# A two-layer graph transformer on one core: chain tiles, one standing PSUM tile, and sums by identity products

## The chip, the cores and the metric

The kernel runs on one core of a Trainium2 chip. The metric is the device time of one execution in microseconds, with all operands and the result in device memory. A matrix engine (TensorE, PE in the profile), a vector engine (VectorE, DVE), an activation engine (ScalarE, ACT), GpSimd (POOL) and the queues of SyncE (SP) work side by side, each in its own order, and wait for one another by semaphores. Tiles lie in SBUF or in PSUM; PSUM has eight banks of 512 floats per partition, and matrix products land there.

## The reference

2500 nodes with 128 features and one of 16 types, 40,000 edges with one of 32 types. Two layers of typed attention, a linear output with bias, the old features added, and a last normalisation:

```python
k, q, v = typed_linear(x, ntype, Wk | Wq | Wv).reshape(n, H=8, HS=16)
kT = einsum('nhd,htdo->nhto', k, Watt)      # every node, every edge type
vT = einsum('nhd,htdo->nhto', v, Wmsg)
a  = einsum('ehd,ehd->eh', kT[src, :, etype], q[dst]) * pri[:, etype].T / 4
att = edge_softmax(a, dst, n)               # over the edges of one target node
hag = segment_sum(vT[src, :, etype] * att[:, :, None], dst)
h = silu(typed_linear(hag, ntype, Wa)) * alpha + x * (1 - alpha)
x = (h - mean) / sqrt(var + 1e-5) * g + b   # end of a layer
out = layernorm(x0 + x @ ff_w + ff_b)       # after both layers
```

A typed linear takes for each node the matrix of the node's type.

## The kernel before

**Preparation.** The edges are ranked by target and type on the chip, and the nodes are sorted by in-degree into 49 blocks of 128. In a block every node has as many slots as the largest in-degree there (25, 21, 19, ... 11 in four classes of four node types, and 42 (written TOP; 26 own slots and a remainder that several rows share), 20, 16, 14, 9 for a mixed rest of all types). A table in DRAM, `tab`, holds one row of k and v (256 floats) per node and edge type.

**A layer** is `edges(l)`. For every slot of a block POOL issues one indirect DMA (L1528) that gathers 128 rows of the table, one for each node of the block. Four slots fill one chunk, a `kv` tile of [128, 4, 256]; there are twelve such tiles, and a gather waits until the chunk that used its tile twelve chunks ago has been read for the last time. When a chunk has landed, DVE multiplies its k half by the block's query (L1544, "kk") and sums over each head (L1550), which gives the scores `a`. When all chunks of a block have their scores, the generator `finished` does the rest in steps, mixed into the chunks of the next block (three steps to a chunk): mask, maximum and subtraction on DVE, exp on ACT, the sum of the weights (`den`), then for every chunk v times weight and the addition to `acc`, and last a reduction of `acc` over its four slots to `sums`.

In layer 0 query and `acc` lie in SBUF and the weights in one PSUM bank (`hold`). In layer 1 the query is copied by ACT (L1353) into a double bank of the pool `tps`, where the weights and `acc` lie as well; the profile calls that tile `tb`.

**Superblocks.** Up to four blocks form a superblock. After its last block `nodes` follows: normalise the sums, typed linear, tanh, skip and layer norm. A typed linear takes DVE masks (`masked`: xm = (type == t) x h^T) and a PE product for each type, into a PSUM bank of the pool `nps` (tiles `nb`). In layer 0 `nodes` also makes k, v and q of the next layer and then `table_block`, which makes the second layer's table rows: PE products (L354) into double banks of `tps`, copies to `st` tiles by ACT and DVE (L362, L360), and a scatter by POOL (L1761). In layer 1 it makes the output rows, which POOL scatters (L1793). `queries0` makes the queries of the next superblock in layer 0; `queries1` loads them in layer 1.

**Order.** POOL's order is that of the program: gathers and scatters as written. For DVE, ACT and PE a scheduler keeps the program's order nearly, with hints by which nothing is pulled ahead of the chunk at hand (`Held`; instructions issued through it all have line 267 in the profile). `spread` and `tick` hand out the steps of `nodes`, of the queries and of the tables to the slots: so many steps for so many slots, where the number of steps is written in the program. A scatter is put behind by eight steps (`late`).

PSUM before: one bank for `nps`, one for `hold`, three double banks for `tps`, eight banks in all.

## Time and profile before

| | |
|---|---|
| median of 3 runs | 3025.17 us (3024.95 to 3028.88) |
| the profiled execution's own time | 3024.62 us |
| its span, first to last instruction | 3022.8 us |
| preparation | 0 to 590 us |
| layer 0, first to last gather | 590 to 1803 us |
| passage: last rows of the second table | 1803 to 1874.6 us |
| layer 1 | 1874.6 to 2976.5 us |
| tail after the last gather | 2976.5 to 3022.8 us |
| busy over the span | PE 52%, DVE 63%, ACT 32%, POOL 67% |

Times are read against the execution's own 3024.62 us; the 1.8 us beside the span lie before the first and after the last instruction. A row of the groups gives line, engine, operation, tile written <- tiles read, shapes, count, then busy us, mean ns, and the idle time just ahead of these instructions with what ended it. In a row of the timeline the bracket at the end is the idle time ahead. "issue" means that nothing the profile shows was waited for. A PE product in float32 has two records.

### The profile page before, as it was taken

The numbers are of one execution on the slowest core, as the hardware profiler recorded it, in microseconds if no ns is written. First come the engines' busy times: TensorE is split into PE (matmuls) and PEld (weight loads), VectorE is DVE, ScalarE is ACT, GpSimd is POOL, SyncE is SP. The second block draws the span as 40 slices with busy tenths as digits, with TensorE's granted clock in tenths as the row PEclk, the third lists the DMA queues.
The fourth block names the chain that finished last, engine by engine and source line by source line (L and its number), as shares of the span: only waits on it lengthen the run. The fifth ranks groups of instructions, "written<-read, shape, count | busy, mean of one in ns | idle before, by whom it ended". The sixth has DMA issues, their size and how long they took to land.

```text
span 3022.8 us, 21562 instructions
## 1 busy us (share of the span) xinstructions
PE 1580.5 (52%) x5325; PEld 703.1 (23%) x5325; DVE 1891.1 (63%) x4383; ACT 978.7 (32%) x1635; POOL 2032.2 (67%) x2116
## 2 busy tenths in 40 slices
PE   5999978413667667777777884021122213221212
PEld 2445434201223322332223332010111001000001
DVE  7467655257657766777666653476576667666665
ACT  3887533200434234434444553011111111111111
POOL 3333665477777777777777762777677777777773
PEclk9999777556777777787777786555555556555555
DMA  7999999943677577867788897333334333333331
GB/s 217 416 418 418 394 392 397 371 107 100 234 275 260 197 248 282 297 225 254 271 303 296 330 354 278 105 110 111 92 103 118 111 111 109 112 109 106 106 100 45
DMA packets 163485, 671.37 MB, mean 222 GB/s; under 512 B 52012, under 2 KB 78926, under 8 KB 138302
## 3 DMA queue, kind: packets, MB, share of 16 engines
q0 software_dynamic: 113152, 635.19, 58.6%
q1 hardware_dynamic: 34218, 27.57, 3.3%
q10 hardware_dynamic: 15976, 7.10, 1.0%
q8 instruction: 46, 0.75, 0.1%
q14 instruction: 93, 0.76, 0.1%
HBM read 245.42 MB, written 425.02 MB: 222 GB/s over the span
## 4 chain that ended last, share of the span: by engine, by line
POOL 24%; issue 17%; DMA 16%; DVE 13%; PE 7%; ACT 3%; ACTq 0%; DVEq 0%; POOLq 0%
POOL kv L1528 21%; DMA kv<-tab,ell 14%; PE nb L267 6%; DVE kv L1544 2%; DVE xm L267 2%; PE tb L354 2%; DVE kv L267 2%; DMA tab<-st,row 2%; DVE a L1550 1%; DVE acc L267 1%; ACT L267 1%; POOL tab L1761 1%; DVE tb L267 1%; DVE hs L267 1%; POOL out_dram L1793 1%
## 5 line engine op out<-in xcount | busy, mean ns | idle before, releaser
L1528 POOL DMA_INDIRECT kv<-tab,ell x1638 | 1615.6, 986 | 542.6 <-issue 437.4
L362 ACT COPY st<-tb 128x512 f32<-128x512 f32 (+1 forms) x984 | 681.6, 777 | 535.4 <-PE tb L354 349.8
L1544 DVE TENSOR_TENSOR kv<-kv,tb 128x512 f32<-128x512 f32 (+3 forms) x223 | 142.7, 640 | 381.1 <-DMA kv<-tab,ell 367.4
L1544 DVE TENSOR_TENSOR kv<-kv,q 128x512 f32<-128x512 f32 (+3 forms) x223 | 142.9, 643 | 324.6 <-DMA kv<-tab,ell 316.1
L354 PE MATMUL tb<-bdv,vT 32*128 32x512 f32 x784 | 266.0, 781 | 45.0 <-ACT st L362 41.5
L1550 DVE TENSOR_REDUCE a<-kv 128x32 f32<-128x512 f32 (+3 forms) x446 | 280.8, 632 | 1.3
L354 PE MATMUL tb<-bdv,kvT 32*128 32x512 f32 x784 | 253.7, 790 | 22.9 <-ACT st L362 22.5
L354 PE MATMUL tb<-bdk,kvT 32*128 32x512 f32 x784 | 257.3, 776 | 7.9 <-ACT st L362 7.3
L267 PE MATMUL nb<-xm,wa 128*128 128x384 f32 (+2 forms) x336 | 178.0, 690 | 148.8 <-DVE xm L267 144.2
L267 PE MATMUL nb<-xm,wkqv 128*128 128x384 f32 (+2 forms) x504 | 218.6, 583 | 48.0 <-DVE xm L267 37.0
L1168 POOL DMA_INDIRECT tab<-st,rows x98 | 101.8, 1039 | 197.7 <-ACT st L362 169.4
L360 DVE COPY st<-tb 128x512 f32<-128x512 f32 (+1 forms) x192 | 128.7, 707 | 145.3 <-PE tb L354 74.7
L267 PE MATMUL nb<-by,all_rows 49*128 49x512 bf16 (+2 forms) x30 | 13.3, 442 | 381.6 <-DVE by L267 353.5
L354 PE MATMUL tb<-bdk,kT 32*128 32x512 f32 x784 | 210.6, 785 | 1.7 <-issue 1.6
L267 PE MATMUL nb<-ident,hag 128*128 128x128 f32 x98 | 24.6, 385 | 284.1 <-DVE hag L267 276.4
L1761 POOL DMA_INDIRECT tab<-st,row x98 | 106.1, 1083 | 80.4 <-DVE st L360 28.0
L267 PEld LDWEIGHTS nb<-xm,wkqv 128*128 128x128 f32 x504 | 106.4, 223 | 174.8 <-issue 88.6
L267 PEld LDWEIGHTS nb<-xm,wa 128*128 128x128 f32 x336 | 85.9, 272 | 240.6 <-issue 184.3
L267 DVE TENSOR_TENSOR tb<-kv,tb 128x512 f32<-128x512 f32 (+3 forms) x216 | 138.2, 640 | 0.2
L267 PE MATMUL nb<-xm,wq 128*128 128x384 f32 (+2 forms) x168 | 92.0, 708 | 87.2 <-DVE xm L267 87.1
L354 PEld LDWEIGHTS tb<-bdv,vT 32*128 32x128 f32 x784 | 98.8, 226 | 147.7 <-ACT st L362 118.9
L1353 ACT COPY tb<-hq 128x128 f32<-128x128 f32 x49 | 13.0, 267 | 369.4 <-DVE sums L267 268.8
(348 smaller groups left out, 2519.9 us busy)
## 6 DMA issues: line engine op xcount, KB each, us to landing
kv<-tab,ell POOLq DMA_INDIRECT x1638
hq<-hqx SPq DMA_DIRECT2D x7, 768.0 KB, 4.8
hqx<-hs SPq DMA_DIRECT2D x7, 512.0 KB, 3.5
hq<-hqx SPq DMA_DIRECT2D x5, 576.0 KB, 4.9
hqx<-xr SPq DMA_DIRECT2D x10, 256.0 KB, 19.2
hqx<-hs SPq DMA_DIRECT2D x5, 384.0 KB, 3.2
hr<-hqx SPq DMA_DIRECT2D x7, 256.0 KB, 5.6
tab<-st,rows POOLq DMA_INDIRECT x98
```

The lines of the kernel that those rows point to most:

```text
L267: put = issue(*args, **kwargs)
L354: stream[nc.tensor] = nc.tensor.matmul(pt[:, b], yT[s, i * P:(i + 1) * P], bd[s, tt, :], start=True, stop=True)
L360: nc.vector.tensor_copy(to, pt)
L362: stream[nc.scalar] = nc.scalar.copy(to, pt)
L1168: put = nc.gpsimd.indirect_dma_start(out=tabs[0].rearrange("(n t) c -> n (t c)", t=16), out_offset=bass.IndirectOffsetOnAxis(ap=rows1[:, t ...
L1353: nc.scalar.copy(pair[:, 1, :D], got[s][0][:, i, :])
L1528: get = nc.gpsimd.indirect_dma_start(out=kv[:, j - j0, :], out_offset=None, in_=tabs[l][:], in_offset=bass.IndirectOffsetOnAxis(ap=ell[:, ...
L1544: stream[nc.vector] = nc.vector.tensor_tensor(kk, kk, of.unsqueeze(1).to_broadcast([P, c, D]), op=ALU.mult)
L1550: nc.vector.tensor_reduce(to, kk.rearrange("p k (h d) -> p k h d", h=H), axis=AX.X, op=ALU.add)
L1761: put = nc.gpsimd.indirect_dma_start(out=tabs[1].rearrange("(n t) c -> n (t c)", t=16), out_offset=bass.IndirectOffsetOnAxis(ap=row2[:, tg ...
L1793: put = nc.gpsimd.indirect_dma_start(out=out, out_offset=bass.IndirectOffsetOnAxis(ap=node[:, b:b + 1], axis=0), in_=o[:, i, :], in_offset ...
```

## The change

PSUM is dealt out anew: two banks for `nps` (before, one), two double banks for `tps` (before, three), and one standing tile `held` of two banks for both layers. Its first bank is `acc`; its second holds the weights in front and two places for queries, used in turn, behind.

- Both layers: ACT copies the block's query into `held` (L1351; in layer 0 this is a new copy); exp writes the weights there. The widest block keeps its weights in SBUF, but its sums go to `held` too.
- Layer 0: `acc` moves from SBUF to `held`; DVE still multiplies and adds.
- Layer 1: DVE multiplies v by the weights in place, chunk by chunk, and PE adds up: a product of the chunk with the identity into `held`, with start at the block's first chunk and stop at its last. DVE's additions are gone.
- `linear_of` no longer copies h^T to SBUF for a mixed superblock: the masks read PSUM.
- In layer 0's mixed superblocks k, v and q are made in two passes over the masks, (k, v) and (q), where it was three.
- The steps handed to `spread` go from 58 extra to 41, from 14 to 13, and from 25 to 24.

```diff
--- before.py
+++ after.py
@@ -315,11 +315,6 @@
         types = list(types)
-        if len(types) > TC:
-            h2 = pool.tile([P, SB * P], F32, name="h2", tag="hb")
-            on.scalar.copy(h2[:, :n], hT[:, :n])
-            yield
-            hT = h2
         some, ps = 2 if len(types) > TC else TC, None
         for t0 in range(0, len(types), some):
             xms = list(masked(pool, types[t0:t0 + some], ntb, hT, n))
@@ -1214,10 +1209,14 @@
         eps = npl.tile([P, 1], F32, name="eps")
         nc.vector.memset(eps, LN_EPS)
-        nps = ctx2.enter_context(tc.tile_pool(name="nps", bufs=1 if fast else 5, space=PSUM))
-
-        hold_ps = ctx2.enter_context(tc.tile_pool(name="hold", bufs=1, space=PSUM)) if fast else None
-        tps = ctx2.enter_context(tc.tile_pool(name="tps", bufs=3, space=PSUM))
+        nps = ctx2.enter_context(tc.tile_pool(name="nps", bufs=2 if fast else 5, space=PSUM))
+
+        turn, held = [0], None
+        if fast:
+            hold_ps = ctx2.enter_context(tc.tile_pool(name="hold", bufs=1, space=PSUM))
+            held = hold_ps.tile([P, 2, SB * P], F32, name="held")
+            assert max(OWN, *KB[:TOP], *KB[TOP + 1:]) * H <= 2 * D
+        tps = ctx2.enter_context(tc.tile_pool(name="tps", bufs=2 if fast else 3, space=PSUM))
         sbs = []
@@ -1347,22 +1346,20 @@
             def query(s, i):
-                if l == 0:
-                    return got[s][0][:, i, :], None
-                pair = tps.tile([P, 2, SB * P], F32, name="tb")
-                nc.scalar.copy(pair[:, 1, :D], got[s][0][:, i, :])
-                return pair[:, 1, :D], pair
-
-            def moved(pair, by, what, to):
+                at = (2 + turn[0] % 2) * D
+                turn[0] += 1
+                nc.scalar.copy(held[:, 1, at:at + D], got[s][0][:, i, :])
+                return held[:, 1, at:at + D]
+
+            def moved(by, what, to):
                 n = what.shape[1]
-                ps = pair[:, 1, D:D + n] if pair is not None else tps.tile(
-                    [P, 2, SB * P], F32, name="tb")[:, 0, :n]
+                ps = tps.tile([P, 2, SB * P], F32, name="tb")[:, 0, :n]
                 nc.tensor.matmul(ps, by, what, start=True, stop=True)
                 nc.scalar.copy(to, ps)
-            def finished(s, i, chunks, kvt, a, pair, sums, den):
+            def finished(s, i, chunks, kvt, a, sums, den):
                 i0, k, _ = sbs[s]
@@ -1371,7 +1368,7 @@
                 rest = None
                 if i0 + i == TOP:
                     rest, chunks = kvt[-1], chunks[:-1]
-                    moved(pair, node_of, rest[:, 3, :RK * REST * H],
+                    moved(node_of, rest[:, 3, :RK * REST * H],
                           a[:, OWN:K, :].rearrange("p k h -> p (k h)"))
                     yield
                 on.vector.tensor_tensor(
@@ -1386,24 +1383,29 @@
                 yield
                 w = av
                 if rest is None:
-                    if l == 0:
-                        held = hold_ps.tile([P, SB * P], F32, name="hold")
-                    w = (pair[:, 1, D:D + K * H] if l else held[:, :K * H]).rearrange(
-                        "p (k h) -> p k h", h=H)
+                    w = held[:, 1, :K * H].rearrange("p (k h) -> p k h", h=H)
                 on.scalar.activation(w, av, AF.Exp)
                 if rest is not None:
-                    moved(pair, rows_of, a[:, OWN:K, :].rearrange("p k h -> p (k h)"),
+                    moved(rows_of, a[:, OWN:K, :].rearrange("p k h -> p (k h)"),
                           rest[:, 3, :RK * REST * H])
                 yield
                 yield
                 on.vector.tensor_reduce(den[:, i, :], w.rearrange("p k h -> p h k"),
                                         axis=AX.X, op=ALU.add)
-                if rest is None and l:
-                    acc = pair[:, 0].rearrange("p (k c) -> p k c", k=CH)
-                else:
-                    acc = ep.tile([P, CH, D], F32, name="acc", bufs=1)
+                acc = held[:, 0].rearrange("p (k c) -> p k c", k=CH)
                 wide = acc.shape[1]
-                for j in range(len(chunks) + 1):
+                for j, (j0, j1) in enumerate(chunks if l else []):
+
+                    c = j1 - j0
+                    v = kvt[j][:, :c, D:]
+                    vh = v.rearrange("p k (h d) -> p k h d", h=H)
+                    on.vector.tensor_tensor(
+                        vh, vh, w[:, j0:j1, :].unsqueeze(3).to_broadcast([P, c, H, HS]),
+                        op=ALU.mult)
+                    on.tensor.matmul(acc[:, :c], ident, v, start=(j == 0),
+                                     stop=(j == len(chunks) - 1))
+                    yield
+                for j in range(0 if l else len(chunks) + 1):
                     if j < len(chunks):
                         j0, j1 = chunks[j]
                         v = kvt[j][:, :j1 - j0, D:]
...
@@ -1450,7 +1452,7 @@
                                             op=ALU.add)
                 if i == k - 1:
                     spread(work, nodes(l, *sbs[s], sums, den, *got[s][1:], lambda gen: table(s, gen)),
-                           (42 if l else 33) + (0 if len(sbs[s][2]) == TC else 14 if l else 58),
+                           (42 if l else 33) + (0 if len(sbs[s][2]) == TC else 13 if l else 41),
                            room(s))
             def asking(s):
...
@@ -1680,16 +1682,17 @@
                     yield
                     table(None)
                     outs = []
-                    for j in range(3):
-                        outs.append(nps.tile([P, SB * P], F32, name="nb"))
+                    for js in ((0, 1), (2,)):
+                        outs += [nps.tile([P, SB * P], F32, name="nb") for _ in js]
                         for t0 in range(0, TY, 2):
                             xms = list(masked(npl, types[t0:t0 + 2], ntb, h2, n))
                             yield
                             for t, xm in xms:
-                                on.tensor.matmul(outs[j][:, :n], wkqv[:, j, t, :], xm[:, :n],
-                                                 start=(t == 0), stop=(t == TY - 1))
+                                for j in js:
+                                    on.tensor.matmul(outs[j][:, :n], wkqv[:, j, t, :], xm[:, :n],
+                                                     start=(t == 0), stop=(t == TY - 1))
                             yield
-                        if j < 2:
+                        for j in js[:2 - js[0]]:
                             to = npl.tile([P, SB * P], F32, name=f"kvT{j}", bufs=2)
                             on.scalar.copy(to[:, :n], outs[j][:, :n])
                             outs[j] = to
```

How it moves instructions is shown at three places. The first is layer 1's last block but one beside the last one's scores, on DVE. Before (kv<-kv,tb from L1544 is kk, from L267 v times weight, tb<-kv,tb the first product or an addition):

```order
L267 TENSOR_TENSOR kv<-kv,tb 128x4x128
L1544 TENSOR_TENSOR kv<-kv,tb 128x4x128 [waits DMASW6_49,DMASW7_49,DMASW5_49,DMASW0_49]
L267 TENSOR_TENSOR tb<-kv,tb 128x512 [waits DVE_49]
L267 TENSOR_TENSOR t<-rs 128x2 [waits Activation_49]
L1550 TENSOR_REDUCE a<-kv 128x32 [waits DVE_49]
L267 TENSOR_TENSOR t<-t,v 128x2 [waits DVE_49]
L267 TENSOR_TENSOR kv<-kv,tb 128x4x128
L267 SCALAR_TENSOR_TENSOR rs<-t,rs 128x2 [waits DVE_49]
L1544 TENSOR_TENSOR kv<-kv,tb 128x4x128 [waits DMASW3_49,DMASW4_49,DMASW2_49,DMASW1_49]
L267 SCALAR_TENSOR_TENSOR hs<-hs,rs,bt 128x128 [waits DVE_49]
```

After, at the corresponding chunks:

```order
L267 TENSOR_TENSOR kv<-kv,held 128x4x128 [waits PE_49]
L267 TENSOR_TENSOR t<-rs 128x2 [waits Activation_49]
L267 TENSOR_TENSOR t<-t,v 128x2 [waits DVE_49]
L267 SCALAR_TENSOR_TENSOR rs<-t,rs 128x2 [waits DVE_49]
L267 TENSOR_TENSOR kv<-kv,held 128x4x128 [waits PE_49]
L1546 TENSOR_TENSOR kv<-kv,held 128x4x128 [waits DMASW6_49,DMASW5_49,DMASW7_49,DMASW0_49,PE_49]
L267 TENSOR_TENSOR kv<-kv,held 128x4x128
L267 TENSOR_SCALAR o<-nb,mv,rs 128x128 [waits DVE_49]
L267 TENSOR_SCALAR o<-nb,mv,rs 128x128
L1552 TENSOR_REDUCE a<-kv 128x32 [waits DVE_49]
L267 TENSOR_TENSOR kv<-kv,held 128x4x128 [waits PE_49]
L267 TENSOR_TENSOR kv<-kv,held 128x128 [waits PE_49]
```

The additions between the products are gone, and the products and kk wait for PE where they waited for nothing or for DVE itself.

The second is the last block's sums in layer 1 on DVE, where only the end of the program follows. Before:

```order
L267 TENSOR_TENSOR tb<-kv,tb 128x512 [waits DVE_49]
L267 TENSOR_TENSOR kv<-kv,tb 128x4x128 [waits DVE_49]
L267 TENSOR_TENSOR tb<-kv,tb 128x512 [waits DVE_49]
L267 TENSOR_TENSOR kv<-kv,tb 128x4x128 [waits DVE_49]
L267 TENSOR_TENSOR tb<-kv,tb 128x512 [waits DVE_49]
L267 TENSOR_TENSOR kv<-kv,tb 128x128 [waits DVE_49]
L267 TENSOR_TENSOR tb<-kv,tb 128x512 [waits DVE_49]
L267 TENSOR_TENSOR tb<-kv,tb 128x128 [waits DVE_49]
L267 TENSOR_REDUCE sums<-tb 128x128 [waits DVE_49]
L267 TENSOR_TENSOR hag<-sums,rd 128x256 [waits DVE_49]
```

After, on DVE, and then the same block's products on PE:

```order
L267 TENSOR_REDUCE den<-held 128x8 [waits Activation_49]
L267 TENSOR_TENSOR kv<-kv,held 128x4x128
L267 RECIPROCAL rd<-den 128x16 [waits DVE_49]
L267 TENSOR_TENSOR rd<-rd,nonempty 128x16 [waits DVE_49]
L267 TENSOR_TENSOR kv<-kv,held 128x4x128 [waits PE_49] x4
L267 TENSOR_TENSOR kv<-kv,held 128x128 [waits PE_49]
L267 TENSOR_REDUCE sums<-held 128x128 [waits PE_49]
L267 TENSOR_TENSOR hag<-sums,rd 128x256 [waits DVE_49]
```

```order
L267 MATMUL held<-kv,ident 128x512 [waits DMASW1_49,DMASW2_49,DMASW0_49,DMASW3_49,DVE_49,Activation_49]
L267 MATMUL held<-kv,ident 128x512 [waits DMASW6_49,DMASW5_49,DMASW7_49,DMASW4_49,DVE_49]
L267 MATMUL held<-kv,ident 128x512 [waits DMASW3_49,DMASW2_49,DMASW4_49,DMASW1_49,DVE_49]
L267 MATMUL held<-kv,ident 128x512 [waits DMASW6_49,DMASW5_49,DMASW7_49,DMASW0_49,DVE_49]
L267 MATMUL held<-kv,ident 128x512 [waits DMASW3_49,DMASW2_49,DMASW4_49,DMASW1_49,DVE_49]
L267 MATMUL held<-kv,ident 128x128 [waits DMASW5_49,DVE_49]
```

The block's eleven instructions on DVE (eight of them shown before) have become six, with a PE product behind each; every product but the first waits for PE, and every PE product for DVE.

The third is layer 0 on ACT, the first blocks. Before (hold<-a is exp, q<-nb the end of `queries0`):

```order
L267 ACTIVATE hold<-a 128x144 [waits DVE_49]
L267 ACTIVATE hold<-a 128x136 [waits DVE_49,Activation_49]
L267 ACTIVATE hold<-a 128x128 [waits DVE_49,Activation_49]
L267 CAST ntb<-nb 128x384 [waits PE_49]
L267 ACTIVATE hold<-a 128x120 [waits DVE_49,Activation_49]
L267 COPY qT<-nb 128x384 [waits PE_49]
L267 COPY q<-nb 128x384 [waits PE_49]
L267 ACTIVATE hold<-a 128x120 [waits DVE_49,Activation_49]
```

After:

```order
L267 ACTIVATE held<-a 128x144 [waits Activation_49]
L1351 COPY held<-q 128x128 [waits DVE_49,Activation_49]
L267 ACTIVATE held<-a 128x136 [waits DVE_49,Activation_49]
L1351 COPY held<-q 128x128 [waits DVE_49,Activation_49]
L267 ACTIVATE held<-a 128x128 [waits DVE_49,Activation_49]
L1351 COPY held<-q 128x128 [waits DVE_49,Activation_49]
L267 CAST ntb<-nb 128x384 [waits PE_49]
L267 ACTIVATE held<-a 128x120 [waits DVE_49,Activation_49]
L267 COPY qT<-nb 128x384 [waits PE_49]
L267 COPY q<-nb 128x384 [waits PE_49]
```

Between two exps there is now a query copy, which waits for DVE, and an exp waits for the copy's tile as the copy waits for its.

12 lines of the change are left out of this document (6 added, 6 removed).

## The prediction

> **What bounds the kernel now.** First the span, then the four stages, read from the windows view (columns: stretch, length, then busy time and count of PE, PEld, DVE, ACT and POOL, the granted clock, the DMA share, GB/s).
>
> ```profile
> span 3022.8 us, 21562 instructions
> 590.00:1803.00 1213.00, 830.72 (x2559) 338.72 (x2559) 798.50 (x1749) 468.93 (x635) 930.25 (x908) 0.74 0.71 250
> 1803.00:1874.60 71.60, 43.46 (x167) 18.63 (x167) 28.70 (x59) 29.76 (x40) 9.33 (x9) 0.76 0.80 319
> 1874.60:2976.50 1101.90, 210.75 (x463) 106.29 (x463) 694.10 (x1693) 146.53 (x302) 827.93 (x864) 0.54 0.37 108
> 2976.50:3022.80 46.30, 13.01 (x32) 8.03 (x32) 24.22 (x73) 10.64 (x16) 3.99 (x4) 0.50 0.03 10
> ```
>
> The stages are layer 0, the passage to layer 1, layer 1 and the tail; the 590 us ahead are preparation, which the change leaves alone. In both layers POOL issues one gather per slot, and the timeline says how fast:
>
> ```profile
> 2292.44 0.95 POOL L1528 DMA_INDIRECT kv<-tab,ell  x1 [0.30 <-issue]
> 2293.69 0.94 POOL L1528 DMA_INDIRECT kv<-tab,ell  x1 [0.30 <-DVE a L1550]
> 2293.38 1.27 DVE L267 TENSOR_TENSOR kv<-kv,tb 128x512 f32<-128x512 f32 x2
> ```
>
> A gather takes 0.95 us and 0.30 us of issue. Layer 1: 827.93 + 864 x 0.30 = 1087 of 1101.9 us. Layer 0: 930.25 + 908 x 0.30 = 1203 of 1213. So POOL paces both layers, although no engine's busy share says so. The groups of POOL instructions (layer 0 first, then the passage, then layer 1) show that the gathers differ:
>
> ```profile
> L1528 POOL DMA_INDIRECT kv<-tab,ell x819 | 833.5, 1018 | 270.2 <-issue 215.4 <-ACTq L1959 19.6 <-DMA kv<-tab,ell 11.2
> L1761 POOL DMA_INDIRECT tab<-st,row x89 | 96.8, 1087 | 29.4 <-issue 21.7 <-ACT st L362 5.4 <-DMA kv<-tab,ell 1.1
> L1761 POOL DMA_INDIRECT tab<-st,row x9 | 9.3, 1036 | 51.1 <-DVE st L360 28.0 <-ACT st L362 17.1 <-issue 4.2
> L1528 POOL DMA_INDIRECT kv<-tab,ell x819 | 782.1, 955 | 272.4 <-issue 222.1 <-DVE t L267 12.8 <-DMA tab<-st,row 12.2
> ```
>
> The same 819 gathers cost 51.4 us more in layer 0. Where, the timeline of POOL and DVE shows:
>
> ```profile
> 1353.63 1.36 POOL L1528 DMA_INDIRECT kv<-tab,ell  x1 [0.30 <-issue]
> 1355.30 3.56 POOL L1528 DMA_INDIRECT kv<-tab,ell  x1 [0.30 <-DMA kv<-tab,ell]
> 1354.70 1.48 DVE L267 SCALAR_TENSOR_TENSOR xm<-ntb,h 128x384 f32<-128x384 bf16 x3
> 1356.10 0.54 DVE L1544 TENSOR_TENSOR kv<-kv,q 128x384 f32<-128x384 f32 x1
> 1356.57 1.48 DVE L267 SCALAR_TENSOR_TENSOR xm<-ntb,h 128x384 f32<-128x384 bf16 x3
> ```
>
> The 3.56-us gather stands beside an unbroken run of DVE instructions that read two operands from SBUF and ends with it; in layer 1 the partner of kv lies in PSUM (tb) and gathers beside it keep 0.94 to 0.95 us. Load of the DMA engines is not the cause, by two 60-us windows of layer 0:
>
> ```profile
> 1000.00:1060.00 60.00, 47.00 (x169) 24.42 (x167) 44.86 (x103) 16.89 (x23) 48.11 (x40) 0.83 0.55 189
> 1480.00:1540.00 60.00, 49.02 (x154) 18.12 (x154) 38.16 (x87) 32.78 (x44) 45.98 (x47) 0.74 0.83 299
> ```
>
> At DMA share 0.83 POOL issues 47, at 0.55 only 40.
>
> **The change, part by part.** *Layer 0, operands to PSUM.* The groups of DVE instructions:
>
> ```profile
> L1544 DVE TENSOR_TENSOR kv<-kv,q 128x512 f32<-128x512 f32 (+3 forms) x221 | 141.9, 645 | 323.2 <-DMA kv<-tab,ell 314.7 <-ACT q L267 7.6 <-issue 0.6
> L267 DVE TENSOR_TENSOR acc<-kv,acc 128x512 f32<-128x512 f32 (+3 forms) x168 | 105.3, 627 | 0.1
> L267 DVE SCALAR_TENSOR_TENSOR xm<-ntb,h 128x256 f32<-128x256 bf16 (+1 forms) x160 | 71.1, 483 | 14.2 <-PE nb L267 9.5 <-ACT h L267 4.0
> L267 DVE TENSOR_REDUCE sums<-acc 128x128 f32<-128x512 f32 x47 | 48.9, 1041 | 0.1
> ```
>
> These three kinds with two SBUF operands are 141.9 + 105.3 + 71.1 = 318 us. The first two move to PSUM; of 160 masks 64 stay, 64 x 0.44 = 28 us, or 9%. Removable at most: 51.4 of the gathers and 89 x (1087 - 1036) ns = 4.5 of the scatters, 56 us; less 9%, 51. Fewer masks and a shorter reduction (1041 ns here, 678 in layer 1's row below) save DVE time too, but DVE waits 323 us for gathers, so I cost that at nothing.
>
> Against it: 49 more query copies on ACT (0.27 us each, row below; 13 us beside 469 of 1213, on an engine with room), a double bank fewer for the table products (3 to 2), and kk waiting for exp and query copy, because `held` is one tile. What could come late is st, and behind it a scatter at POOL, with all gathers behind that. One late scatter costs about 5.7 us (51.1/9 in the passage's row). None: 51. Half of layer 0's 14 superblocks: 51 - 7 x 5.7, some 11. The rows (5.4 us on ACT for 89 scatters) are nearer to none; I take not quite two, **-42** (-51 to -11).
>
> ```profile
> L1353 ACT COPY tb<-hq 128x128 f32<-128x128 f32 x49 | 13.0, 267 | 369.4 <-DVE sums L267 268.8
> ```
>
> One rule bears here: the Trainium skill, SBUF — State Buffer, section "Who interferes with whom", says that a DVE instruction with two SBUF inputs contends with a GpSimd instruction that reads SBUF, and one with at most one SBUF input does not; the 1018 against 955 ns agree. The same section infers that tensor_tensor leaves descriptor generation alone; by that sentence this part would gain nothing (rival E).
>
> *The passage.* `nb` gains a bank, the table products lose one; the one change can bring its scatters forward and the other put them back: 0, and no more than one late scatter, 5.7 us, either way.
>
> *Layer 1, sums on PE.* The groups of layer 1 and its tail, then from the timeline a product of the same size and a small one that DVE waits for:
>
> ```profile
> L267 DVE TENSOR_TENSOR tb<-kv,tb 128x512 f32<-128x512 f32 (+3 forms) x216 | 138.2, 640 | 0.2
> L267 DVE TENSOR_REDUCE sums<-tb 128x128 f32<-128x512 f32 x48 | 32.5, 678 | 0.0
> L267 DVE BATCH_NORM_STATS2 bn<-nb 128x6 f32<-128x128 f32 x49 | 11.2, 285 | 17.4 <-PE nb L267 17.2
> 2410.35 2.08 PE L267 MATMUL nb<-hq,ident 128*128 128x512 f32 x2
> 2996.84 0.66 PE L267 MATMUL nb<-ident,hag 128*128 128x128 f32 x2 [14.36 <-DVE hag L267]
> 2997.54 1.41 DVE L267 SCALAR_TENSOR_TENSOR xm<-ntb,nb 128x256 f32<-128x256 bf16 x4 [0.85 <-PE nb L267]
> ```
>
> Of the 216, 48 are first products (0.68 us each, 33) and 168 are adds: 105 us, off DVE. In their place PE multiplies each of 223 chunks by the identity: 2.08 us for 512 columns (two records are one product) at the granted 0.54. Since `held` is tracked as a whole, DVE's next product v*w, and the next block's kk, wait until PE has written the sum: 2.08 + 0.19 of hand-over (0.85 waited for 0.66 of work, in the last two rows) = 2.27 us, of which some 0.6 lies behind another DVE instruction (a reduction, a normalisation): 1.67 open. DVE's need: 694 - 105 = 589, waits of the present kind some 45 (17.4 on PE above and about as much on ACT), 223 x 1.67 = 372, and 49 x 1.5 = 74 for exp and query (an estimate: two steps of some 0.3 us, their hand-overs, and half a microsecond in ACT's queue). Sum 1080, POOL 1087. So POOL still paces, by a hair, and the long blocks (four of 25 slots) lack some 0.7 us each: 3. One gather wait exists:
>
> ```profile
> 2181.30 1.22 POOL L1528 DMA_INDIRECT kv<-tab,ell  x1 [11.29 <-DVE t L267]
> ```
>
> It ends when DVE frees the first kv buffer of the widest block; now PE must have read it too: +2. Together **+5**. Bounds: -2 (that wait shrinks, since DVE has less queued ahead) and +29 (nothing covers: 8 blocks of 21 and 25 slots x 6 products x 0.6).
>
> *The tail.* Nothing hides the last block's six products:
>
> ```profile
> 2975.48 0.94 POOL L1528 DMA_INDIRECT kv<-tab,ell  x1 [0.30 <-DVE rs L267]
> 2988.48 0.70 DVE L267 TENSOR_TENSOR tb<-kv,tb 128x512 f32<-128x512 f32 x1
> 2995.54 0.69 DVE L267 TENSOR_REDUCE sums<-tb 128x128 f32<-128x512 f32 x1
> 3016.93 0.98 POOL L1793 DMA_INDIRECT out_dram<-o,node  x1 [27.02 <-DVE o L267]
> ```
>
> Before: 2995.54 - 2988.48 = 7.06 us. After: 5 x (0.65 + 2.27) + 0.28 + 0.7 = 15.6. With something for the block ahead of it **+9**; at full clock a product is 1.04 + 0.19, and the phase 10.4: +3. At the other end +12, one more product for the block ahead. The rows say half clock (0.50 in the tail, with DVE between all products). The Trainium skill, TensorE: Matmul & The Clock Gate, section "Part 1: The HAM clock gate", lets the clock rise only after about 3.4 us of sustained work; by it too the gaps of 0.65 us decide, +9 if they count as idle, +3 if not, and no run here shows this pattern.
>
> **Sum:** -42 + 0 + 5 + 9 = -28 against the profiled execution's own 3024.62 us (span 3022.8), that is 2996.6; the median of the runs is 0.55 higher: **2997**.
>
> **The rivals.**
> A, the forecast: 0.55. Its own range is 2983 to 3011, half the way to the good bounds of the four parts (-14), and as much on the other side.
> B, nothing is lost: PE stays warm, every product is covered, no scatter is late: -51 + 0 + 3 = -48, 2977. For it: PE idles 80% of layer 1. Against: DVE has little of its own to put between products. 0.18.
> C, scatters set layer 0's pace: ACT copies st in a queue with 49 more steps that wait for DVE: -11 + 5 + 9 = +3, 3028. For it: PE at 49 of 60 us in 1480 to 1540. Against: the 5.4 us above. 0.11, and spread towards A.
> D, slower: DVE becomes layer 1's bound by turns with PE on `held`. It decides where the open wait per product passes (1087 - 589 - 45 - 74)/223 = 1.7 us; at 1.9 DVE needs 1132, 45 more than POOL: 3025.2 - 42 + 45 + 9 = 3037. For it: only 0.03 us of margin per product. Against: part of each wait falls where DVE waits for gathers. 0.12.
> E, the long gathers have another cause than DVE's operands, and layer 0 gains nothing: 3025.2 + 14 = 3039. For it: layer 0 also moves more than twice the data (250 against 108 GB/s). Against: the two 60-us windows. 0.04; the skill's inferred sentence would make it likelier.
>
> **How the numbers follow.** Range 2973 to 3030: it leaves out most of D (0.09), E (0.04), a third of C (0.04) and the low end of B (0.03), 0.2 in all. A change under 0.2% (6 us) cannot be told from none. Faster: A and B whole, 0.03 of C: 0.76. Same: 0.06 of C, 0.02 of D: 0.08. Slower: 0.10 of D, E, 0.02 of C: 0.16.
>
> **What would show it.** Right: the layer-0 gather at 950 to 965 ns, 46 or more POOL instructions in 1000 to 1060; in layer 1 v*w with some 1.5 us of idle time ahead released by PE, yet hardly a gather released by DVE or PE; first to last of the v products of the tail 14 to 16 us. Wrong: a gather mean still above 1000 ns (E); scatters idle on st for more than 20 us (C); layer-1 gathers idle on DVE or PE for more than 30 us (D); PE clock near 1 in layer 1 (B).

## The result, and the profile after

The changed kernel takes 2999.36 us (median of 4 runs, 2998.16 to 3002.62) against 3025.06 us of the kernel before (4 runs): a ratio of 0.9913, 95% interval 0.99 to 0.9926. The forecast was 2997 us. Its profiled execution took 2999.74 us, with this span and, from the windows view, these stages (columns as before the change):

```profile
span 2997.7 us, 22873 instructions
```

```profile
594.50:1759.10 1164.60, 905.38 (x2539) 356.53 (x2540) 780.51 (x1712) 480.78 (x676) 876.28 (x908) 0.71 0.74 260
1759.10:1845.00 85.90, 64.18 (x189) 26.11 (x188) 31.99 (x63) 35.83 (x50) 8.90 (x11) 0.60 0.70 277
1845.00:2943.60 1098.60, 556.29 (x900) 203.63 (x900) 618.62 (x1537) 148.10 (x299) 824.47 (x864) 0.58 0.37 108
2943.60:2997.70 54.10, 25.92 (x42) 10.01 (x40) 19.22 (x55) 7.20 (x11) 4.02 (x5) 0.53 0.03 9
```

Against the stages of before, cut at the first and last gather of each layer:

| stage | before | after | difference | forecast |
|---|---|---|---|---|
| preparation | 591.7 | 594.5 | +2.8 | 0 |
| layer 0 | 1210.3 | 1164.6 | -45.7 | -42 |
| passage | 72.6 | 85.8 | +13.2 | 0 |
| layer 1 | 1101.8 | 1098.7 | -3.1 | +5 |
| tail | 46.4 | 54.1 | +7.7 | +9 |
| sum | 3022.8 | 2997.7 | -25.1 | -28 |

A second profile of the same kernel (the control below) has 592.1, 1167.1, 85.7, 1099.7 and 51.2 us: the preparation's 2.8 us, which the change does not touch, is the scatter between executions, and of the tail's 54.1 some 3 us are too.

**Layer 0 and layer 1 on POOL.** The groups of gathers and scatters, first layer 0, then layer 1, then the passage:

```profile
L1530 POOL DMA_INDIRECT kv<-tab,ell x819 | 785.2, 959 | 273.6 <-issue 210.2 <-ACTq L1962 20.3 <-DMA kv<-tab,ell 8.5
L1764 POOL DMA_INDIRECT tab<-st,row x89 | 91.1, 1024 | 35.0 <-issue 17.4 <-ACT st L357 11.4 <-DMA kv<-tab,ell 2.4
L1530 POOL DMA_INDIRECT kv<-tab,ell x819 | 778.8, 951 | 268.9 <-issue 238.2 <-PE held L267 15.2 <-DMA tab<-st,row 8.5
L1764 POOL DMA_INDIRECT tab<-st,row x9 | 8.8, 983 | 68.5 <-DVE st L355 37.1 <-ACT st L357 20.2 <-issue 5.9
```

A gather of layer 0 fell from 1018 to 959 ns, nearly layer 1's. The stretch that had 40 POOL instructions now has 48, while DVE does more there:

```profile
1000.00:1060.00 60.00, 49.08 (x163) 21.68 (x162) 49.09 (x114) 26.67 (x40) 45.68 (x48) 0.83 0.67 233
```

**Layer 1 and tail on DVE.** The groups of kk, of v times weight and of the reduction to `sums` in layer 1 and tail:

```profile
L1546 DVE TENSOR_TENSOR kv<-kv,held 128x512 f32<-128x512 f32 (+3 forms) x223 | 142.2, 640 | 275.3 <-DMA kv<-tab,ell 130.2 <-PE held L267 124.1 <-ACT held L1351 8.2
L267 DVE TENSOR_TENSOR kv<-kv,held 128x512 f32<-128x512 f32 (+3 forms) x216 | 137.6, 637 | 129.8 <-PE held L267 129.7
L267 DVE TENSOR_REDUCE sums<-held 128x128 f32<-128x512 f32 x49 | 33.7, 688 | 33.3 <-PE held L267 33.3
```

The last block's products on DVE and PE, from the timeline:

```profile
2956.57 0.68 DVE L267 TENSOR_TENSOR kv<-kv,held 128x512 f32<-128x512 f32 x1
2962.28 0.69 DVE L267 TENSOR_TENSOR kv<-kv,held 128x512 f32<-128x512 f32 x1 [2.17 <-PE held L267]
2963.02 2.07 PE L267 MATMUL held<-kv,ident 128*128 128x512 f32 x2 [0.78 <-DVE kv L267]
2965.13 0.69 DVE L267 TENSOR_TENSOR kv<-kv,held 128x512 f32<-128x512 f32 x1 [2.17 <-PE held L267]
2972.02 0.69 DVE L267 TENSOR_REDUCE sums<-held 128x128 f32<-128x512 f32 x1 [0.89 <-PE held L267]
```

DVE and PE take turns: 0.69 us of product, 2.07 us of sum, and neither works while the other does. From the first product to the reduction 2972.02 - 2956.57 = 15.45 us, where it was 7.06.

**The passage.** Where before POOL's scatters stood 2.6 to 5.8 us apart (but for one long wait in the middle), they now stand 5.2 to 6.9 us apart, and the timeline of PE shows why. First before, then after (eight records are two of the four groups of one scatter), and last, from the windows, six microseconds of the latter:

```profile
1808.28 2.04 PE L354 MATMUL tb<-bdv,kvT 32*128 32x512 f32 x8
1810.11 2.04 PE L354 MATMUL tb<-bdk,kvT 32*128 32x512 f32 x8
```

```profile
1769.45 1.84 PE L349 MATMUL tb<-bdk,kvT 32*128 32x512 f32 x4 [0.22 <-ACT st L357]
1773.62 4.09 PE L349 MATMUL tb<-bdk,kvT 32*128 32x512 f32 x8
1776.88 4.04 PE L349 MATMUL tb<-bdv,kvT 32*128 32x512 f32 x8
1780.10 4.04 PE L349 MATMUL tb<-bdk,kvT 32*128 32x512 f32 x8
```

```profile
1775.00:1781.00 6.00, 6.00 (x16) 2.01 (x16) 5.69 (x12) 3.62 (x5) 0.98 (x1) 0.50 0.86 366
```

Before, eight records every 1.83 us, at a granted clock of 1.00 (windows 1803 to 1815); after, every 3.24, without a gap, at 0.50. PE had waited twice for ACT to empty one of its two places (0.39 and 0.22 us), its clock fell, and from then on it was itself the slowest, with 6.00 of 6.00 us busy. That these two waits brought the clock down is argued: before, PE waits for ACT at the same place too (0.25 and 0.59 us, at 1806.44 and 1813.89), and its clock falls as well, but some microseconds later (0.60 in 1815 to 1821).

The larger part of the loss lies in the last four scatters. Here are the first and the fourth of them with six microseconds between, first before, then after:

```profile
1850.11 0.97 POOL L1761 DMA_INDIRECT tab<-st,row  x1 [26.46 <-DVE st L360]
1861.41 0.97 POOL L1761 DMA_INDIRECT tab<-st,row  x1 [4.17 <-issue]
1851.00:1857.00 6.00, 5.45 (x32) 1.70 (x28) 3.58 (x3) 2.63 (x3) 1.79 (x3) 1.00 0.93 393
```

```profile
1814.99 0.97 POOL L1764 DMA_INDIRECT tab<-st,row  x1 [25.31 <-DVE st L355]
1835.54 0.97 POOL L1764 DMA_INDIRECT tab<-st,row  x1 [5.89 <-issue]
1823.00:1829.00 6.00, 5.89 (x16) 2.01 (x16) 2.45 (x2) 1.55 (x3) 0.32 (x1) 0.50 0.82 350
```

From the first of the four to the last it took 11.3 us and now takes 20.6; PE gets through 32 records in six microseconds at clock 1.00 and through 16 at 0.50. The five scatters ahead lost 5.3 us.

### The profile page after: what moved, and what is told of

Read it like the earlier page. It is cut to its first block, busy times and chain, and to the rows that moved or that the text cites. A ratio compares the mean times of both kernels' runs of the same rounds, so it can differ in the third digit from the quotient of the medians.

```text
span 2997.7 us, 22873 instructions
## 1 busy us (share of the span) xinstructions
PE 2032.8 (68%) x5771; PEld 826.6 (28%) x5771; DVE 1797.0 (60%) x4177; ACT 995.3 (33%) x1678; POOL 1973.0 (66%) x2116
## 4 chain that ended last, share of the span: by engine, by line
PE 19%; POOL 15%; issue 12%; DVE 6%; DMA 4%; ACT 4%; DVEq 0%; POOLq 0%; ACTq 0%
POOL kv L1530 14%; PE nb L267 9%; PE tb L349 7%; PE held L267 3%; DMA kv<-tab,ell 3%; ACT st L357 2%; DVE kv L1546 1%; DVE kv L267 1%; ACT L267 1%; DMA tab<-st,row 1%; POOL out_dram L1796 1%; DVE xm L267 1%; DVE a L1552 1%; DVE hs L267 0%; DVE held L267 0%
## 5 line engine op out<-in xcount | busy, mean ns | idle before, releaser
L1530 POOL DMA_INDIRECT kv<-tab,ell x1638 | 1564.1, 955 | 542.5 <-issue 448.4
L267 PE MATMUL held<-kv,ident 128*128 128x512 f32 (+3 forms) x446 | 382.9, 958 | 343.5 <-DVE kv L267 214.2
L1546 DVE TENSOR_TENSOR kv<-kv,held 128x512 f32<-128x512 f32 (+3 forms) x446 | 284.2, 640 | 490.6 <-DMA kv<-tab,ell 273.4
L349 PE MATMUL tb<-bdk,kvT 32*128 32x512 f32 x784 | 296.4, 886 | 46.1 <-ACT st L357 45.9
L267 DVE TENSOR_TENSOR kv<-kv,held 128x512 f32<-128x512 f32 (+3 forms) x384 | 242.1, 631 | 131.0 <-PE held L267 129.7
L349 PE MATMUL tb<-bdv,kvT 32*128 32x512 f32 x784 | 287.0, 900 | 42.8 <-ACT st L357 42.4
L267 PEld LDWEIGHTS held<-kv,ident 128*128 128x128 f32 x446 | 103.2, 285 | 602.6 <-DVE kv L267 368.8
L267 PE MATMUL nb<-xm,wkqv 128*128 128x384 f32 (+2 forms) x504 | 205.7, 563 | 9.9 <-DVE xm L267 9.7
L267 PE MATMUL nb<-xm,wa 128*128 128x384 f32 (+2 forms) x336 | 182.3, 704 | 42.2 <-DVE xm L267 42.2
L267 DVE SCALAR_TENSOR_TENSOR xm<-ntb,nb 128x512 f32<-128x512 bf16 (+2 forms) x304 | 156.9, 562 | 36.2 <-PE nb L267 33.9
L1351 ACT COPY held<-hq 128x128 f32<-128x128 f32 x49 | 13.1, 268 | 448.1 <-DVE sums L267 392.3
L267 DVE TENSOR_TENSOR held<-kv,held 128x512 f32<-128x512 f32 (+3 forms) x222 | 143.6, 647 | 4.1
L267 PEld LDWEIGHTS nb<-xm,wkqv 128*128 128x128 f32 x504 | 104.7, 216 | 121.2 <-issue 46.6
L267 PEld LDWEIGHTS nb<-xm,wa 128*128 128x128 f32 x336 | 88.6, 277 | 141.9 <-DVE xm L267 77.9
```

Of the source, the lines that this page charges most:

```text
L267: put = issue(*args, **kwargs)
L349: stream[nc.tensor] = nc.tensor.matmul(pt[:, b], yT[s, i * P:(i + 1) * P], bd[s, tt, :], start=True, stop=True)
L1351: nc.scalar.copy(held[:, 1, at:at + D], got[s][0][:, i, :])
L1530: get = nc.gpsimd.indirect_dma_start(out=kv[:, j - j0, :], out_offset=None, in_=tabs[l][:], in_offset=bass.IndirectOffsetOnAxis(ap=ell[:, ...
L1546: stream[nc.vector] = nc.vector.tensor_tensor(kk, kk, of.unsqueeze(1).to_broadcast([P, c, D]), op=ALU.mult)
```

## The experiments

Two chips took part. The first comparison above and the runs of the second group ran where the kernel before takes 3025 us. The first and the third group ran on another chip, on which the kernel before itself takes 3374 (first) and 3409 us (third), and engines stand idle in both layers in ways that the profile doesn't name: of the idle time of DVE in the kernel with two tiles 415 us (419 in a second profile) are put to "remote" there, in the kernels profiled here none. The kernel before was timed there, but not profiled. Total times of the two chips aren't compared below. What is compared across them is the mean length of a gather, the passage and the last block's sums, which agree nearly: with two double banks and no third place the passage lies at 85.0 to 89.0 us in six of the seven profiles on that chip (97.3 in the seventh), and at 85.7 and 85.8 here (81.0 where layer 0 is longer, below).

### First group: the passage and the tail, each alone

Two double banks alone, in the kernel before:

```diff
-        tps = ctx2.enter_context(tc.tile_pool(name="tps", bufs=3, space=PSUM))
+        tps = ctx2.enter_context(tc.tile_pool(name="tps", bufs=2 if fast else 3, space=PSUM))
```

> The kernel before with one edit: two double banks for the table products where it has three. Theory (the passage between the layers grew from 72.6 to 85.8 us because PE has one double bank less to write table products to): passage 82 to 88 us here too, all else within 3 us, time +10 to +14 us. Rival (the passage grew from another part of the change: nb's second bank, the standing tile, or the preparation's 2.8 us): passage 70 to 76 us, time within 4 us of before.

Measured: ratio to the kernel before on the same chip 1.0155 (1.0092 to 1.0218), +50 us. Where most of it lies can't be told, as no profile shows the kernel before on that chip. The passage from the windows (the clock stands third from the end), and two of its products from the timeline:

```profile
2010.76:2099.75 88.99, 62.06 (x187) 24.54 (x187) 29.90 (x61) 34.76 (x49) 8.88 (x10) 0.62 0.67 266
```

```profile
2022.82 3.83 PE L354 MATMUL tb<-bdv,kvT 32*128 32x512 f32 x8
2026.00 3.83 PE L354 MATMUL tb<-bdk,kvT 32*128 32x512 f32 x8
```

PE is busy for 62 us where the kernel before, on the other chip, needs 44, at 0.62 of its clock for 0.76, and eight records take 3.2 us again. Nothing else of the change is in this kernel, and its layer 0 isn't shorter (1418.6 us). So the theory's stage came out, a microsecond above its range and by a comparison across chips; the rest of its forecast can't be read on this chip.

The standing tile cut in two:

```diff
-            held = hold_ps.tile([P, 2, SB * P], F32, name="held")
+            held = hold_ps.tile([P, SB * P], F32, name="held")
+            added = hold_ps.tile([P, SB * P], F32, name="added")
...
-                acc = held[:, 0].rearrange("p (k c) -> p k c", k=CH)
+                acc = added.rearrange("p (k c) -> p k c", k=CH)
```

> The changed kernel with the standing tile cut into two tiles of one bank each, the sums in one, weights and queries in the other; nothing else. Theory (v times weight waits for PE only because sums and weights are tracked as one tile): DVE's 130 us of waits on PE ahead of v times weight and 124 ahead of kk fall below 20 each, the last block's products go from 15.4 us to 9 to 12 (PE's own six products, 5 x 2.08 + 0.8 at half clock, less if PE warms up), tail 54.1 to 48 to 51, time -3 to -6 us against the changed kernel; layer 1 stays at 1099 +/- 2 since POOL paces it. Rival (the waits also hold layer 1's gathers up): layer 1 gets shorter too, by 5 us or more.

Measured: 3447.73 us, ratio 1.0212 to the kernel before there. The tail is 43.1 us, below the forecast of 48 to 51; the waits for PE ahead of v times weight are gone. What it does for layer 1 can't be told on a chip where POOL isn't the pace (1279 us).

Layer 1's sums on DVE:

```diff
-                for j, (j0, j1) in enumerate(chunks if l else []):
+                for j, (j0, j1) in enumerate([]):
...
-                for j in range(0 if l else len(chunks) + 1):
+                for j in range(len(chunks) + 1):
```

> The changed kernel with layer 1's sums added up by DVE, as in its layer 0, and no identity products; nothing else. Theory (the identity products cost the tail 7.7 us and bring layer 1 nothing, since POOL paces it): tail 46 to 47.5 us, last block's products 7 us, layer 1 1097 to 1102, time -6 to -9 us against the changed kernel. Rival (DVE's relief is what made layer 1 3.1 us shorter): layer 1 1102 or more, time within 4 us of the changed kernel.

Measured: 3445.36 us, ratio 1.0202; tail 49.5 us, above its range of 46 to 47.5, but 9 us below the 58.7 us of the kernels on this chip that have one tile and PE's sums. A third place for table products:

```diff
...
+                    if w == 2 and thirds:
+                        thirds.append(thirds.pop(0))
+                    pt = thirds[0] if w == 2 and thirds else None
+                    if pt is None:
+                        pt = ps_pool.tile([P, w, SB * P], F32, name="tb")
...
+            if fast and l == 0:
+                thirds.extend([None, None, held])
             while work or pieces or late:
...
```

> The changed kernel; once the last block of layer 0 is done, every third group of table products is written to the standing tile, which is idle then, in place of the double banks of their own; nothing else. Theory (a third place to write to keeps two groups of products on PE at once and its clock up): passage 85.8 to 72 to 78 us, granted clock in the passage above 0.70 (it is 0.60), time -8 to -13 us against the changed kernel. Rival (the passage is longer because less of the table is left of layer 0's work, or by chance): passage above 83 us, time within 4 us.

Measured: 3469.82 us, ratio 1.0276; passage 79.5 us, granted clock there 0.69 (85.0 to 86.3 us and 0.60 to 0.64 in the changed kernel's other variants without it on this chip). So the stage gains some 6 us and the clock rises, as the theory has it, but both stop short of its marks (72 to 78 us, above 0.70), and the tail stays long (58.7 us). On this chip no total could be tested, so edits that touch different stages were put together for the next group.

### Second group: on the chip of the first comparison

The control:

> The changed kernel as it is, as the control beside the edits on one chip. On a chip like that of the first comparison: 2998 to 3003 us, passage 86, tail 54. On one like that of the four edits before, where the kernel before took 3374 us: whether the change is a gain there at all is open; theory (its engines stand still for other reasons there, so that POOL is not the pace): no gain, 3390 us or more; rival (the gain of layer 0 is POOL's and holds everywhere): 3350 or less.

Measured: 2998.34 us, ratio 0.9907 (0.9883 to 0.993), the first result again.

Layer 0's operands back to SBUF:

```diff
             def query(s, i):
+                if l == 0:
+                    return got[s][0][:, i, :]
...
-                acc = held[:, 0].rearrange("p (k c) -> p k c", k=CH)
+                acc = (held[:, 0].rearrange("p (k c) -> p k c", k=CH) if l else
+                       ep.tile([P, CH, D], F32, name="acc", bufs=1))
```

> The changed kernel with layer 0's query and sums back in SBUF (no query copy there); weights, masks, banks and layer 1 as changed. Theory (the layer-0 gathers were long because DVE read two operands from SBUF): gather mean in layer 0 from 959 back to 1000 to 1012 ns, layer 0 +35 to +44 us against the changed kernel where POOL paces it. Rival (the shorter mask passes or the second nb bank shortened layer 0): gather mean under 970 ns, layer 0 within 8 us of the changed kernel.

Measured: 3030.47 us, ratio 1.0017 (1.0006 to 1.0029): all of the change's gain is gone, and a little more. Layer 0 takes 1199.7 us, 32.6 more than the control, by its gathers (first the control, then this kernel):

```profile
L1530 POOL DMA_INDIRECT kv<-tab,ell x819 | 786.3, 960 | 272.1 <-issue 211.4 <-ACTq L1962 19.4 <-DVE held L267 7.1
L1533 POOL DMA_INDIRECT kv<-tab,ell x819 | 822.1, 1004 | 270.8 <-issue 212.0 <-ACTq L1965 19.6 <-DMA kv<-tab,ell 8.5
```

822.1 - 786.3 = 35.8 us. The gathers' mean is in the theory's range, layer 0's 32.6 us are a little below its 35 to 44: three quarters of layer 0's 43 us are the two operands. The passage is 4.7 us shorter here (81.0), so some of what layer 0 gains seems to be given back there, since with gathers that end sooner more of the table is left to be made. That was a rival of the third-place run, and it has a part.

Two tiles and a third place, where the two banks of the standing tiles take the third group, with a copy for each bank:

```diff
...
-            held = hold_ps.tile([P, 2, SB * P], F32, name="held")
+            held = hold_ps.tile([P, SB * P], F32, name="held")
+            added = hold_ps.tile([P, SB * P], F32, name="added")
...
+            if fast and l == 0:
+                thirds.extend([None, None, (added, held)])
...
```

> The changed kernel with the standing tile cut in two (sums; weights and queries), and with every third group of table products written to these two banks once the last block of layer 0 is done. Theory (the tail pays for one tile, the passage for two double banks): tail 54 to 43 to 48 us, passage 86 to 74 to 80, layer 1 within 2 us, time -14 to -22 us against the changed kernel. Rival (either loss has another cause): that stage stays within 3 us.

Measured: 2967.54 us (2966.5 to 2970.43), ratio 0.9811 (0.9794 to 0.9827): 31 us below the control and 58 below the kernel before. Passage 77.0, layer 1 1093.3, tail 36.7 us, ten below the kernel before and below the forecast of 43 to 48. In the passage the third place doesn't hold the clock up from the start: it is 0.50 from 1763 to 1799, and the first five scatters take 27.1 us for the changed kernel's 24.2. The gain lies in the last four, 11.6 us for 20.6, where the clock is 1.00 (1805 to 1817) for 0.50. The last block's products and sums, DVE, PE, and the reduction:

```profile
2933.62 3.27 DVE L267 TENSOR_TENSOR kv<-kv,held 128x512 f32<-128x512 f32 x6
2934.35 6.66 PE L267 MATMUL added<-kv,ident 128*128 128x512 f32 x12 [7.01 <-DVE kv L267]
2941.04 0.69 DVE L267 TENSOR_REDUCE sums<-added 128x128 f32<-128x512 f32 x1 [3.79 <-PE added L267]
```

DVE multiplies six chunks in one run of 3.27 us, PE adds behind it without a gap, six sums in 6.66 us, where by turns at half clock they take 5 x 2.07 + 0.80 = 11.2. Part of that is the missing gaps, part the clock: the windows view has it at 0.50 up to 2938.0 and at 1.00 from 2939.5, so it comes up some 4 us after PE began with the first sum. First product to reduction: 7.42 us, for 15.45. DVE waits 0.0 us ahead of v times weight in layer 1:

```profile
L267 DVE TENSOR_TENSOR kv<-kv,held 128x512 f32<-128x512 f32 (+3 forms) x210 | 131.0, 635 | 0.0
```

The sums on DVE with a third place:

> The changed kernel with layer 1's sums added up by DVE in the standing tile (no identity products), and with every third group of table products written to the standing tile once the last block of layer 0 is done. Theory (identity products bring layer 1 nothing, as POOL paces it, and cost the tail): tail 46 to 48 us, layer 1 1098 to 1102, passage 74 to 80, time -13 to -21 us against the changed kernel. Rival (DVE's relief shortened layer 1): layer 1 +3 us or more, and the time above that of the kernel with two tiles by as much.

Measured: 2974.41 us (2971.39 to 2978.81), ratio 0.9833 (0.9815 to 0.9852). Passage 79.8, layer 1 1091.4, tail 41.3 us. Both expectations were wrong on layer 1: it is neither within 2 us of the control nor longer without PE's sums, but 6.4 (two tiles) and 8.3 us (DVE) shorter. The waits of POOL say where. Between the gathers of layer 1 the changed kernel, like the kernel before, has one long one, 11.56 us at the widest block; in both of these kernels there is none of 2 us. The timeline of POOL, DVE and PE of the changed kernel at that place:

```profile
2120.80 0.43 DVE L1546 TENSOR_TENSOR kv<-kv 128x256 f32<-128x256 f32 x1 [18.55 <-DMA kv<-tab,ell]
2151.90 0.94 POOL L1530 DMA_INDIRECT kv<-tab,ell  x1 [11.56 <-PE held L267]
2121.92 0.68 DVE L267 TENSOR_TENSOR kv<-kv,held 128x512 f32<-128x512 f32 x1
2124.77 0.69 DVE L1546 TENSOR_TENSOR kv<-kv,held 128x512 f32<-128x512 f32 x1 [2.17 <-PE held L267]
2145.07 0.69 DVE L267 TENSOR_TENSOR kv<-kv,a 128x512 f32<-128x512 f32 x1
2145.09 1.64 PE L267 MATMUL nb<-ffb,one_row 1*128 1x384 f32 x2
2147.15 1.49 PE L267 MATMUL nb<-hq,ident 128*128 128x384 f32 x2
2148.43 1.49 PE L267 MATMUL nb<-ffw,h 128*128 128x128 f32 x6
2149.71 3.46 PE L267 MATMUL held<-kv,ident 128*128 128x512 f32 x5
```

DVE loses some microseconds to PE on its way to the widest block's first product, and once that is there (2145.07) its sum stands behind the output products in PE's queue until 2149.71; only then is the kv tile free for POOL. In the kernel with DVE's sums the same first product comes 20 us after the remainder's chunk (2114.60) where it was 24 (2120.80), and the next gather leaves one microsecond later, where it was seven:

```profile
2114.60 0.43 DVE L1552 TENSOR_TENSOR kv<-kv 128x256 f32<-128x256 f32 x1 [19.57 <-DMA kv<-tab,ell]
2134.56 0.69 DVE L267 TENSOR_TENSOR held<-kv,a 128x512 f32<-128x512 f32 x1
2135.52 0.94 POOL L1536 DMA_INDIRECT kv<-tab,ell  x1 [1.52 <-DVE held L267]
```

So it seems that the change without the alternation of DVE and PE would have taken the old wait away, and that one tile together with PE's sums put a new one of nearly the same size in its place; that layer 1 was no longer than before hid it. This is argued, not shown, in one point: both kernels without the wait also have the third place, and no run on this chip has one edit without the other. How the passage, which ends some 300 us ahead of that wait, could remove it the traces don't show.

### Third group: the parts of layer 0, and repeats

This group fell on the other chip again; the runs tell by the gather's length and the passage alone.

> The kernel before with two double banks for the table products in place of three, once more, on a chip on which POOL paces it. Theory (two double banks keep fewer groups of products on PE at once, its clock falls, and the passage grows): passage 72.6 to 79 to 86 us, granted clock there below 0.68 (0.76 before), layer 0 within 4 us of 1210, time +6 to +14 us. Rival (the passage of the changed kernel is long only because a shorter layer 0 leaves more of the table to make): passage 70 to 75 us, time within 3 us.

Measured: 3470.35 us, ratio 1.0194 (1.0154 to 1.0234); passage 97.3 us at a clock of 0.58, PE busy for 67.0 us; gathers 1019 ns. The theory's direction came out once more, its size (79 to 86) did not, and layer 0 is disturbed (1458 us), so that the condition of this run, a chip on which POOL sets the pace, was not met.

> The changed kernel with the standing tile cut in two (sums; weights and queries), without the third place for table products. Theory (one tile costs the tail and the wait at the widest block): tail 36 to 38 us, layer 1 1092 to 1095, passage 85 to 87 as in the changed kernel, time -18 to -24 us against it (2998). Rival (some of the kernel with both edits' gain in tail and layer 1 came from the earlier end of the passage): layer 1 above 1097 or tail above 42.

Measured: 3476.78 us, ratio 1.0206 (1.0171 to 1.024). First product to reduction of the last block 3447.55 to 3454.79, 7.24 us, nearly as with both edits (7.42); passage 86.3, as expected without the third place. Layer 1 (1278.6) and tail (47.8) carry the chip's idle times, so whether the wait at the widest block goes with two tiles alone remains open; that it goes with two tiles and a third place is shown.

The query alone back in SBUF, and then the masks alone as before (with the number of steps handed to `spread` that belongs to them):

> The changed kernel with layer 0's query alone back in SBUF; the sums stay in PSUM. Theory (each kind of instruction with two SBUF operands costs the gathers by its busy time): 142 of 247 us, so 57% of the 32.6 us that query and sums together bring: layer 0 1167 to 1183 to 1188 us, gather mean 980 to 988 ns. Rival (the runs of several such instructions count, not their time, and the sums' additions make the runs): less than a third, layer 0 under 1178.

> The changed kernel with the mixed superblocks' masks as before: three passes for k, v and q, and h^T copied to SBUF for the query's; all else as changed. Theory (masks read from SBUF hold gathers up too): the part of layer 0's gain that query and sums do not explain, 43 - 33 = 10 us, comes back: layer 0 1167 to 1174 to 1180 us, gather mean 968 to 976 ns. Rival (the masks are too few and beside too few gathers; the rest is the shorter reduction or scheduling): layer 0 under 1171.

The group of layer 0's gathers, first with the query in SBUF, then with the masks as before:

```profile
L1532 POOL DMA_INDIRECT kv<-tab,ell x819 | 810.2, 989 | 341.5 <-issue 223.2 <-DVE held L267 46.7 <-ACTq L1964 20.5
```

```profile
L1535 POOL DMA_INDIRECT kv<-tab,ell x819 | 788.3, 963 | 360.5 <-issue 223.8 <-DVE held L267 60.6 <-DVE kv L1551 22.0
```

Beside kernels with both operands in PSUM (959 to 963 ns on either chip) the query costs some 27 ns a gather, 61% of the 44 that both cost: near the share of its busy time (57%), as the theory has it, though a nanosecond above its range, and not under a third. With the masks alone the gather, at 963 ns, stays within the scatter of those kernels: there the rival is right. Layer 0's own length can't be read in either run (1437.9 and 1474.4 us on this chip). What is left, 1018 - 1004 = 14 ns or 11 us in all, belongs to neither alone. Masks beside kk and additions, as in the 3.56-us gather of the prediction, would fit, but no run put the masks back together with query and sums, and it stays open.

Every kernel of this chip that has the change in it, with the query in SBUF too, is 2.0 to 2.8% slower than the kernel before there; the changed kernel itself did not run on it. Where POOL isn't the pace, shorter gathers bring nothing, and the change has more steps that one engine waits for another in. That this is the reason is only argued.

## Why the prediction was right, and where not

The time came out right (2997 against 2999.36), by sums that were right in two stages and wrong in two whose errors, +13.2 and -8.1, partly cancel; of what is left of them, 5.1 us, layer 0's -3.7 and the tail's -1.3 take the rest. That the total is only 2.4 us off is therefore luck; that the time fell by layer 0's gathers is not.

- **What bounds the kernel.** POOL paces both layers: in layer 0 876.28 + 908 x 0.30 = 1149 of 1164.6 us, in layer 1 824.47 + 864 x 0.30 = 1084 of 1098.7.
- **Layer 0, -42: right, -45.7 and -43.2.** Gathers and scatters lost 48.3 + 5.7 = 54 us (the forecast: 51), and late st and other waits rose from 1210.3 - 1202.7 = 7.6 to 1164.6 - 1148.7 = 15.9, 8 us (the forecast: 9). Of layer 0's 43 to 46 us the query and sums are shown to be 33. The 9% for the masks that stay was a share by busy time; masks alone are shown to matter less. The prediction has the 3.56-us gather end with the run of two-operand instructions beside it; by its own rows the gather ends at 1358.86 and the run shown at 1358.05, so that one gather proves less than it says, and the runs with the operands moved back have to carry the cause.
- **The passage, 0: wrong, +13.2.** The step that failed is the price of the lost double bank. I priced it in late scatters of 5.7 us, taken from a passage with three places, and put no more than one of them in the bounds. The runs show in its place that two places slow the table products themselves: in the changed kernel PE is busy 64 us for 44 in the passage, at 0.60 of its clock for 0.76, and 62 us at 0.62 with that edit alone (on the other chip). A third place brought 6 us back on either chip with one tile, and 8.7 with two tiles. The clearest measure is the last four scatters, from the start of the first to that of the last: 20.5 to 20.6 us in all ten profiles with two places, 11.3 to 11.6 in all four with three, on both chips. That is 9.2 of the 13.2 us. The other 4 lie ahead of them, where the kernel with query and sums in SBUF is 4.9 us shorter than the control, so that they seem to belong to the shorter layer 0; a run that shows it alone is missing.
- **Layer 1, +5: wrong in sign, -3.1 and -2.1.** The balance held: DVE waited 129.7 + 124.1 + 33.3 = 287 us for PE (the forecast: 372), and POOL stayed the pace. The sign named for it, some 1.5 us ahead of each v times weight, did not come: there it is 129.8 / 216 = 0.6 us, and nearly as much lies ahead of kk. The long blocks lost nothing that shows. The wait at the widest block grew by 0.3 us, not 2, and gathers were 4 ns shorter, 3.3 us in all, which I had not in the sum. What I missed altogether is that this wait could go: layer 1 is 6 to 8 us shorter in the two kernels without the alternation, which have the third place too.
- **The tail, +9: right, +7.7 (and +4.8 in the control).** A turn of product and sum is 2.85 us (2965.13 - 2962.28; the forecast: 2.92), the phase 15.45 us (15.6), 8.4 more than before; the rest of the tail is 0.7 (control: 3.6) us shorter.
- **The rivals.** B's premise that PE stays warm is excluded for the changed kernel (0.58 in layer 1, 2.07 us for a sum); in the kernel with two tiles the clock comes up within the last block. C: the scatters of layer 0 waited 11.4 us for ACT, under the 20 set for it. D: no gather waited for PE but at one block. E: excluded by the run with query and sums in SBUF. Of the section "Who interferes with whom" of the Trainium skill's SBUF — State Buffer the inference that tensor_tensor leaves descriptor generation alone does not hold for these gathers (1004 against 960 ns, and 989 with the query alone); the rule on two SBUF inputs agrees with them.

## What to carry to other kernels

Ask of every tile that several engines share what it is tracked as: one tile for sums and weights made DVE and PE take turns, and cutting it in two, without one instruction less, took the last block's phase from 15.45 to 7.24 us. A gain is to be sought where the pacing engine works, and by its own instruction times: the 0.06 us less for a gather, 819 times, is more than the whole gain of this change. And a pool that gives a buffer away is to be priced with the clock of the engine that fills it, not only with its waits.

## What the runs showed of the hardware

- An indirect DMA's issue on POOL got longer beside DVE instructions with two SBUF operands, the more so the more of them there were: 1018 ns on average with all of the kernel before, 1004 with query and sums, 989 with the query alone, 959 to 963 with neither.
- PE worked without a gap for 14 us (1773 to 1787) on products of 32 rows, and the granted clock stayed at 0.50; with six gapless products of 128 rows it came up some 4 us after the first had begun. The rows alone don't decide: in the kernel before products of 32 rows ran at 1.00 from 1803 to 1815. The Trainium skill, TensorE: Matmul & The Clock Gate, "Part 1: The HAM clock gate", has the clock rise after some 3.4 us of sustained work; the second case agrees, the first doesn't. What else the gate looks at no run here tells.
- The same kernel took 3025 us on one chip and 3374 to 3409 on another; in the kernels profiled there layer 1's gathers (952 to 957 ns, here 951 to 955) and kk (636 to 639 ns, here 640 to 643) have nearly the same length as in those profiled here, and what is longer is idle time. Variants of the changed kernel were 2.0 to 2.8% slower than the kernel before there, where the changed kernel is 0.9% faster here. What holds the engines up there is open.
